# A third output buffer for the Mamba scan, room for it from constants moved into a dead tile, and the first scan unit one place sooner in the issue table

## The chip, the cores and the metric

One core of a Trainium2 chip runs the whole kernel. The metric is device microseconds for one execution; the kernel before takes 7903.27 us (median of 3 runs, 7898.69 to 7904.27).

## The reference, cut to what matters

Four layers follow each other on an image of 2 x 64 x 96 x 96 in fp32. Layer 0 is a non-local attention block over all 9216 positions. Layer 1 is a depthwise and pointwise convolution followed by one Mamba over the 9216 positions of each image. Layer 2 runs two bidirectional Mambas, first along the columns, then along the rows, each with a linear map and a residual. Layer 3 is a dynamic 3 x 3 filter. The Mamba of layers 1 and 2 is this, per sequence:

```python
xz = jnp.einsum('nld,ed->nle', u, p['in_proj_w'])
x, z = jnp.split(xz, 2, axis=-1)
x = silu(conv1d(x) + conv_b)                      # 4 taps, depthwise
dt, Bm, Cm = jnp.split(x @ x_proj_w.T, [4, 20], axis=-1)
dt = softplus(dt @ dt_proj_w.T + dt_proj_b)
def step(h, inp):                                 # 16 states for each of 128 channels
    dA = jnp.exp(dt_t[:, :, None] * A)
    h = dA * h + dt_t[:, :, None] * B_t[:, None, :] * x_t[:, :, None]
    return (h, jnp.einsum('nds,ns->nd', h, C_t))
y = (ys + x * p['Dp']) * silu(z)
out = y @ out_proj_w.T                            # plus the residual
```

## The kernel before, in words

Layer 0 (`layer0_direct`) runs alone, to about 2660 us. At its beginning, on idle engines, `prepare` builds the tables and the weights of the first Mamba with the tile `scratch_tile` as scratch. Layers 1 and 2 then run as one stream of 120 units (`layers1_2`, `Mamba.run`). A unit is 768 positions of one image and one direction: 24 units for layer 1 (two images of 12, with a carried state), 96 for layer 2, in pairs of a forward and a backward unit which share their norm and end in one common tail. In the list of units, numbered from 0, layer 2 begins at 24, and the even unit of a pair is the forward one.

**A unit's work.** Its preparation is: norm (`norm_centre` in layer 1 only, `norm_square`, `norm_mean`, `norm_root`, `norm_scale`, `norm_affine`), `conv`, `conv_read`, `gate_mm`, `gate_read`, `silu` (which switches ACT's function table and back), `step_mm`, `step_read`, `step_exp`, then on POOL `step_kept`, `step_sum`, `step_dt`, `step_u`, and `step_write`, which writes the rows of `dt` and `dt*x` to DRAM. `c_mm` and `c_read` make `C`. The scan has 16 steps. A step takes two of the 16 turns of one half of the positions: SP reads its rows back (`read`, L846, five steps ahead, six buffers `spread`), ACT makes the decay (`decay`, L853, three steps ahead, nine buffers `h`), DVE makes the inputs for two steps at once from `spread` and `B` (`inputs`, L863, into `place`), DVE scans (L878, or L874 with a carried state), POOL multiplies by `C` (L879), and PE gathers into the PSUM bank `y` (L885 for the direct term, L888 for the steps) two or three steps later. `B` is one PSUM bank, made anew by `shared` (L857) for each half of a unit: before step 0 and at step 6 for step 8.

**The end of a unit.** `y_half` (L892) copies the first half of `y` from PSUM into the tile `yg`, `y_read` (L895) the second, POOL gates it (`y_gate`, L898). `tail_0` and `tail_1` (L671, one for each half) multiply the `yg` of all units of a group by the output weights on PE, and `tail_read` (L921 or L924) reads the sum. In layer 2 the tail of a pair reads the `yg` of both units, and comes 25 and 26 steps after the start of the second. All PSUM products but `B`, `y` and `place` go through one buffer, tag `m` of the pool `ssm_m`, named `mm` or `conv` in the profile.

**What sets the order.** The order is written out by hand (`manual_schedule`): in `run`, `n` counts steps, 16 to a unit, and for each `n` the pieces of all units whose offset in `PIECES` falls there are issued. So unit `i` has its `conv` at step 16i - 27, its `step_write` at 16i - 6, its scan at 16i to 16i + 15, its `y_half` at 16i + 10. The pieces of unit 0 before its scan are issued ahead of the loop. Within a step the row read, the decay, the inputs, the scan and the gathers are issued first, then the pieces in `reads`, then the others. `other` issues, twice a unit, the leftover pointwise chunks of layer 1 and the weights of later Mambas. Each engine works its own queue in this order.

**Memory.** The pool `ssm` has two buffers per tag unless `bufs` is given. `k.xa`, the big image tile, is dead during layers 1 and 2, and a `Carver` cuts scratch and weights from it. `turned` (1 KB per partition) and `dtw` (2.5 KB) lie in the constant pool.

Of the kernel before, what the change touches and what calls it, by code (L numbers as in the profile page):

```python
# [19 lines left out]
FP = mybir.dt.float32  # L20
# [5 lines left out]
P = 128  # L26
# [45 lines left out]
def setup(ctx, tc, x, cols, mats, dtw):  # L72

    nc = tc.nc
    const = ctx.enter_context(tc.tile_pool(name="const", bufs=1))
    big = ctx.enter_context(tc.tile_pool(name="big", bufs=1))
    k = SimpleNamespace(tc=tc, nc=nc, const=const)

    k.mats = const.tile([P, NMAT], FP, name="mats")
    k.cols = const.tile([P, NCOL], FP, name="cols")  # L80
    k.dtw = const.tile([DT_RANK, NMAMBA * P], FP, name="dtw")
    first = MAT_AT["g_b"][1]
    nc.scalar.dma_start(out=k.mats[:, :first], in_=mats[:, :first])
    nc.scalar.dma_start(out=k.cols, in_=cols)
    nc.scalar.dma_start(out=k.mats[:, first:], in_=mats[:, first:])
    nc.scalar.dma_start(out=k.dtw, in_=dtw)
    k.xa = big.tile([P, L], FP, name="xa")
    k.xb = big.tile([P, L], FP, name="xb")


    half, step = L // 2, L // 6
    own, other = rows_of(0), rows_of(1)
    for i in range(0, half, step):
        nc.sync.dma_start(out=k.xa[own, i : i + step], in_=x[own, i : i + step])
        nc.sync.dma_start(out=k.xb[other, half + i : half + i + step], in_=x[own, half + i : half + i + step])
    nc.sync.dma_start(out=k.xa[other, :half], in_=x[other, :half])
    nc.sync.dma_start(out=k.xb[own, half:], in_=x[other, half:])
    nc.sync.dma_start(out=k.xa[:, half:], in_=x[:, half:])

    k.ident = const.tile([P, P], FP, name="ident")  # L100
    make_identity(nc, k.ident)

    k.mean_c = const.tile([P, P], FP, name="mean_c")
    nc.vector.memset(k.mean_c, 0.0)
    for b in range(B):
        nc.vector.memset(k.mean_c[rows_of(b), rows_of(b)], 1.0 / C)

    k.mean = const.tile([P, 1], FP, name="mean")
    nc.vector.memset(k.mean, 1.0 / C)
    k.mean = k.mean.to_broadcast([P, P])  # L110
    k.eps = const.tile([P, 1], FP, name="eps")
    nc.vector.memset(k.eps, EPS)
    k.minus = const.tile([P, 1], FP, name="minus")
    nc.vector.memset(k.minus, -1.0)

    k.col = lambda name, rows=slice(0, P): k.cols[rows, COL_AT[name][0] : COL_AT[name][1]]
    k.mat = lambda name, rows=slice(0, P): k.mats[rows, MAT_AT[name][0] : MAT_AT[name][1]]
    return k
# [409 lines left out]
def mamba_tables(k, pool):  # L528

    nc = k.nc
    G = P // 8
    t = SimpleNamespace()

    t.member = pool.tile([P, 8], FP, name="member")
    nc.vector.reduce_sum(t.member, k.ident.rearrange("p (g i) -> p i g", i=8), axis=AX.X)
    t.group = pool.tile([P, 2, G], FP, name="group")
    for j in range(2):
        nc.vector.reduce_sum(t.group[:, j], k.ident.rearrange("p (g i) -> p g i", i=8), axis=AX.X)  # L540

    t.turned = pool.tile([P, G, G], FP, name="turned")
    two = t.group.rearrange("p j g -> p (j g)")
    for n in range(G):
        nc.vector.tensor_copy(t.turned[:, n], two[:, G - n : 2 * G - n])

    pair = pool.tile([P, 2, P], FP, name="pair")
    nc.vector.tensor_copy(pair, k.ident.unsqueeze(1).to_broadcast([P, 2, P]))
    pair = pair.rearrange("p j c -> p (j c)")
    t.gather = [pair[:, P - 8 * n : 2 * P - 8 * n] for n in range(G)]  # L550

    t.centre = pool.tile([P, 2, C], FP, name="centre")
    for j in range(2):
        nc.vector.tensor_add(t.centre[:, j], k.ident[:, :C], k.ident[:, C:])
        nc.vector.tensor_scalar_add(t.centre[:, j], t.centre[:, j], -1.0 / C)
    t.centre = t.centre.rearrange("p j c -> p (j c)")
    return t


def scratch(t, pool):  # L560

    t.placed = pool.tile([P, D_STATE, 8], FP, name="placed")
    t.rates = pool.tile([P, P // 8, P // 8], FP, name="turned_rates")


def mamba_weights(k, w, pool, product, tables, i):

    nc = k.nc  # L570
    G = P // 8


    a = pool.tile([P, D_STATE], FP, name=f"A{i}")
    nc.scalar.activation(a, k.col(f"A_log{i}"), AF.Exp)
    nc.vector.tensor_scalar_mul(a, a, -1.0)
    nc.vector.tensor_mul(
        tables.placed,
        tables.member.unsqueeze(1).to_broadcast([P, D_STATE, 8]),
        a.unsqueeze(2).to_broadcast([P, D_STATE, 8]),  # L580
    )
    p = product(tables.placed.rearrange("p s i -> p (s i)"), tables.group[:, 0], P, G)
    yield
    nc.vector.tensor_mul(tables.rates, tables.turned, p.unsqueeze(1).to_broadcast([P, G, G]))  # L584
    w.rates = pool.tile([P, G], FP, name=f"rates{i}")
    nc.vector.reduce_sum(w.rates, tables.rates, axis=AX.X)
    in_w = k.mat(f"in_w{i}")
    if i:
        nc.vector.tensor_scalar_mul(in_w, in_w, k.col(f"norm_w{i}"))
    yield  # L590
    conv_w = k.col(f"convd_w{i}")
    w.taps = pool.tile([P, D_CONV, P], FP, name=f"taps{i}")
    for j in range(D_CONV):
        p = product(conv_w[:, j : j + 1].to_broadcast([P, P]), k.ident, P, P)
        yield
        nc.vector.tensor_mul(w.taps[:, j], in_w[:, :P], p)
        yield
    x_w = k.mat(f"x_w{i}")
    low = pool.tile([DT_RANK, P], FP, name=f"low{i}")
    p = product(x_w[:, :DT_RANK], k.ident, DT_RANK, P)  # L600
    yield
    nc.vector.tensor_copy(low, p)
    yield
    p = product(low, k.dtw[:, bass.ts(i, P)], P, P)
    yield
    w.step = pool.tile([P, P], FP, name=f"step{i}")
    nc.vector.tensor_copy(w.step, p)
    w.direct = pool.tile([P, P], FP, name=f"direct{i}")
    nc.vector.tensor_scalar_mul(w.direct, k.ident, k.col(f"Dp{i}"))
    bc = pool.tile([P, 2, D_STATE, 8], FP, name=f"bc{i}")  # L610
    for j in range(2):
        at = DT_RANK + j * D_STATE
        nc.vector.tensor_copy(bc[:, j], x_w[:, at : at + D_STATE].unsqueeze(2).to_broadcast([P, D_STATE, 8]))
    w.gate_w = in_w[:, P:]
    w.bc = [bc[:, j].rearrange("p s i -> p (s i)") for j in range(2)]
    w.conv_b, w.dt_b = k.col(f"convd_b{i}"), k.col(f"dt_b{i}")
    w.out_w = k.mat(f"out_w{i}")
    yield


class Mamba:
# [33 lines left out]
    def product(self, lhsT, rhs, m, n):  # L655
        p = self.ps_m.tile([P, 2 * NB], FP, tag="m", name="mm")[:m, :n]
        self.nc.tensor.matmul(p, lhsT=lhsT, rhs=rhs, start=True, stop=True)
        return p
# [229 lines left out]
            self.nc.tensor.matmul(self.y, lhsT=self.t.gather[n], rhs=rhs, start=False, stop=stop)  # L888

    def y_half(self, u):  # L890
        u.y = self.work("yg")
        self.nc.scalar.copy(u.y[:, :HALF], self.y)  # L892

    def y_read(self, u):
# [72 lines left out]
    def run(self, units, first, n_first, other):  # L967


        for u in units:  # L970
            u.dtu, u.h = {}, {}
        steps = [(u, s) for u in units for s in range(self.STEPS)]
        at = lambda n: steps[n] if 0 <= n < len(steps) else None
        reads = ("y_half", "norm_square", "norm_root", "conv_read", "gate_read", "step_read", "c_read", "tail_read")

        table = [[] for _ in range(self.STEPS)]
# [16 lines left out]
        for n in range(begin, len(steps) + end + 1):  # L993
# [5 lines left out]
            if at(n):  # L999
                u = at(n)[0]  # L1000


                if s % 2 == 0:
                    self.inputs(u, s)
                    self.inputs(u, s + 1)
                self.scan(u, s)
                if s == 6:
                    self.shared(u, 1)
                if s == 14 and at(n + 2):
                    self.shared(at(n + 2)[0], 0)  # L1010
            if n == -1:
                self.shared(units[0], 0)
            for late in self.lates(s):
                if at(n - late):
                    self.gather(*at(n - late))
            for late in (False, True):
                for is_late, offset, name in table[s]:
                    i = (n - offset) // self.STEPS
                    if is_late == late and (0 if n >= 0 else 1) <= i < len(units):
                        getattr(self, name)(units[i])  # L1020
                if s in self.OTHER and n >= 0 and not late:
                    next(other, None)


def prepare(k, scratch_tile, ps, tag):
# [5 lines left out]
        return p  # L1031

    k.tables = mamba_tables(k, k.const)
    scratch(k.tables, Carver(scratch_tile))
    k.weights = [SimpleNamespace() for _ in range(NMAMBA)]
    for _ in mamba_weights(k, k.weights[0], k.const, product, k.tables, 0):
        pass
# [2 lines left out]
def layers1_2(k, pre):  # L1040
# [12 lines left out]
    with ExitStack() as stack:  # L1053
# [12 lines left out]


        carver = Carver(k.xa)
        scratch(k.tables, carver)

        def joined(which, lin_w, to):

# [239 lines left out]
```

## Time and profile before

The page gives the span of the profiled execution as 7904.9 us. Busy times over that span, and the costliest rows of layers 1 and 2:

| engine or row | count | busy us (share) or mean ns |
|---|---|---|
| PE | 24578 | 7033.6 (89%) |
| DVE | 5524 | 6744.4 (85%) |
| ACT | 6953 | 5205.2 (66%) |
| POOL | 3146 | 4723.5 (60%) |
| scan L878, DVE | 1536 | 1738 ns |
| scan with carry L874, DVE | 768 | 1003 ns |
| inputs L863, DVE | 1920 | 951 ns |
| product with C L879, POOL | 1920 | 1818 ns |
| decay L853, ACT | 3840 | 607 ns |
| gather L888, PE | 7680 | 508 ns |
| read of rows L846, DMA | 3840 | 384 KB each |

The shares over the whole span mix two regimes. Until 2660 us, in the attention, DVE is busy in 6 tenths and POOL hardly at all; in layers 1 and 2 DVE, POOL and the DMA engines show 8 to 9 tenths, and the DMA engines move 315 to 351 GB/s. So a stage has to be looked at by itself. The page's row for a group gives its busy time, the mean of one, and then the idle time of its engine just before such instructions and who ended most of it. An engine's idle time counts for the end only if it is the engine that the others wait for.

### The profile page before, as it was taken

Reading aid. Unit: us, or ns where it says so; the run is one execution under the profiler, and the core shown is the slowest. Engines: PE = TensorE matmul, PEld = TensorE weight load, DVE = VectorE, ACT = ScalarE, POOL = GpSimd, SP = SyncE. Lnnn points to the kernel's source line nnn. Section 1 sums busy time; section 2 is a strip of 40 time slices with the busy share of each in tenths; the row PEclk is TensorE's granted clock in tenths of the full one; section 3 lists DMA queues with packets and bytes.
Section 4 is the critical chain, followed back from the end, with each engine's and each line's share of the span. In section 5 each row is a group of like instructions: output and inputs, shape, how many; then the busy total and the mean of one; then the engine's idle time right before and its main releaser. Section 6 shows DMA issues by size and latency. Waiting matters only on the chain. (4 is left out here: it accounts for less than half of the span.)

```text
span 7904.9 us, 82275 instructions
## 1 busy us (share of the span) xinstructions
PE 7033.6 (89%) x24578; PEld 3098.9 (39%) x24578; DVE 6744.4 (85%) x5524; ACT 5205.2 (66%) x6953; POOL 4723.5 (60%) x3146
## 2 busy tenths in 40 slices
PE   9999999999999798888888888888888888888887
PEld 3333333333333244444444444444444444444443
DVE  6666666666666499999999999999999999999999
ACT  4444444444444587777777777777777777777774
POOL 0000000000000299999888889889889999999995
PEclk9999999999999899999999999999999999999999
DMA  1000000000000299999889899999999999999995
GB/s 43 1 1 1 1 1 1 3 5 5 5 3 5 105 330 322 328 325 329 321 325 333 315 331 334 332 329 337 330 325 351 345 348 347 336 350 342 344 342 209
DMA packets 593806, 1726.06 MB, mean 218 GB/s; under 512 B 65988, under 2 KB 67140, under 8 KB 592840
## 3 DMA queue, kind: packets, MB, share of 16 engines
q1 hardware_dynamic: 591904, 1717.68, 60.4%
q8 instruction: 196, 3.21, 0.2%
q10 hardware_dynamic: 1448, 3.05, 0.1%
q14 instruction: 258, 2.11, 0.1%
HBM read 1522.68 MB, written 197.79 MB: 218 GB/s over the span
## 5 line engine op out<-in xcount | busy, mean ns | idle before, releaser
L879 POOL TENSOR_TENSOR h<-h,C 128x768 f32<-128x768 f32 x1920 | 3454.0, 1818 | 339.2 <-DVE h L878 304.6
L888 PE MATMUL y<-h,pair 128*128 128x384 f32 x7680 | 2803.3, 508 | 135.1 <-POOL h L879 134.5
L878 DVE TENSOR_TENSOR_SCAN h<-h,place 128x768 f32<-128x768 f32 x1536 | 2606.9, 1738 | 10.8 <-ACT h L853 10.7
L888 PEld LDWEIGHTS y<-h,pair 128*128 128x128 f32 x7680 | 1499.1, 199 | 1335.4 <-POOL h L879 297.7
L311 ACT ACTIVATE e<-f_exp 128x1536 f32<-128x1536 f32 x864 | 1206.4, 1448 | 1224.4 <-PE f_exp L301 1224.4
L853 ACT ACTIVATE h<-spread,xa 128x384 f32<-128x384 f32 x3072 | 1722.5, 607 | 395.0 <-DMA spread<-rows 363.4
L367 DVE TENSOR_TENSOR acc_e<-acc_e,e 128x1536 f32<-128x1536 f32 x792 | 1390.2, 1755 | 683.5 <-ACT e L311 644.6
L863 DVE TENSOR_TENSOR place<-spread,B 128x768 f32<-128x768 f32 x1920 | 1735.0, 951 | 199.6 <-PE B L857 126.7
L340 POOL TENSOR_TENSOR xa<-xa,t_att 64x512 f32<-64x512 f32 x36 | 45.3, 1259 | 2612.0 <-ACT t_att L338 2612.0
L318 PE MATMUL y_att<-e,xb 128*64 128x512 f32 x5184 | 1243.6, 601 | 0.0
L301 PE MATMUL f_exp<-theta,phi 64*128 64x512 f32 x5184 | 1234.5, 607 | 1.0 <-DVE xb L284 0.5
L301 PEld LDWEIGHTS f_exp<-theta,phi 64*128 64x128 f32 x5184 | 466.9, 186 | 754.1 <-issue 460.2
L874 DVE TENSOR_TENSOR_SCAN h<-h,state,place 128x384 f32<-128x384 f32 x768 | 716.4, 1003 | 0.0
L318 PEld LDWEIGHTS y_att<-e,xb 128*64 128x64 f32 x5184 | 341.5, 136 | 830.5 <-issue 829.2
L853 ACT ACTIVATE h<-spread,rates 128x384 f32<-128x384 f32 x768 | 433.8, 608 | 90.6 <-DMA spread<-rows 72.8
L885 PE MATMUL y<-raw,xa 128*128 128x384 f32 x384 | 219.0, 659 | 217.2 <-ACT yg L895 189.8
L671 PE MATMUL mm<-raw,xa 128*128 128x384 f32 x768 | 290.6, 502 | 86.0 <-ACT xb L924 85.9
L766 ACT ACTIVATE raw<-conv,cols 128x768 f32<-128x768 f32 x120 | 108.2, 901 | 280.3 <-PE conv L761 218.9
L806 POOL TENSOR_TENSOR kept<-dtu,kept 128x768 f32<-128x768 f32 x120 | 218.2, 1818 | 100.1 <-ACT kept L799 99.8
L761 PE MATMUL conv<-xn,xa 64*128 64x384 f32 (+3 forms) x1536 | 270.2, 490 | 6.9 <-DVE xa L584 3.0
L892 ACT COPY yg<-y 128x384 f32<-128x384 f32 x120 | 57.4, 478 | 290.9 <-PE mm L671 199.4
L857 PE MATMUL B<-raw,xa 128*128 128x384 f32 x384 | 170.7, 526 | 83.9 <-DVE place L863 83.9
(206 smaller groups left out, 5412.2 us busy)
## 6 DMA issues: line engine op xcount, KB each, us to landing
spread<-rows SPq DMA_DIRECT2D x3840, 384.0 KB, 5.6
rows<-dtu SPq DMA_DIRECT2D x240, 768.0 KB, 6.4
image<-pre SPq DMA_DIRECT2D x11, 384.0 KB, 2.3
xb<-image SPq DMA_DIRECT2D x11, 384.0 KB, 6.7
xa<-in_x SPq DMA_DIRECT2D x1, 2304.0 KB, 22.3
out<-xa ACTq DMA_DIRECT2D x7, 240.0 KB, 2.0
out<-xa SPq DMA_DIRECT2D x1, 1200.0 KB
xa<-in_x SPq DMA_DIRECT2D x3, 384.0 KB, 10.9
```

The costliest lines, as they stand in the source:

```text
L301: nc.tensor.matmul(fs[j // 3][:, bass.ts(j % 3, NB)], lhsT=phi[at, bass.ts(m // 2, P)], rhs=theta[at, bass.ts(i, NB)], start=True, stop=True,)
L311: nc.scalar.activation(e, f, AF.Exp)
L318: nc.tensor.matmul(y[rows_of(m % 2)], lhsT=g[:, m, :], rhs=es[j // 3][:, bass.ts(j % 3, NB)], start=m < 2, stop=m >= KEYS - 2,)
L367: nc.vector.tensor_add(acc, acc, e)
L671: self.nc.tensor.matmul(o, lhsT=lhsT, rhs=x, start=n == 0, stop=n == len(terms) - 1)
L761: self.nc.tensor.matmul(p3[:, :, o], lhsT=lhsT, rhs=x3[:, :, i], **flags)
L853: self.nc.scalar.activation(h[:, bass.ts(q, HALF)], dt, AF.Exp, scale=u.w.rates[:, n : n + 1])
L863: self.nc.vector.tensor_mul(bx, x, self.B.unsqueeze(1).to_broadcast([P, 2, HALF]))
L874: nc.vector.tensor_tensor_scan(h[:, at], h[:, at], bx[:, at], state[:, q : q + 1], ALU.mult, ALU.add)
L878: nc.vector.tensor_tensor_scan(h[:, way], h[:, way], bx[:, way], 0.0, ALU.mult, ALU.add)
L879: nc.gpsimd.tensor_mul(h2, h2, u.C[:, bass.ts(half, HALF)].unsqueeze(1).to_broadcast([P, 2, HALF]))
L888: self.nc.tensor.matmul(self.y, lhsT=self.t.gather[n], rhs=rhs, start=False, stop=stop)
```

## The change

Three things change together.

1. `yg`, the output of a unit, gets three buffers instead of two, so that `y_half` of a unit takes the buffer of the third unit back.
2. Room for it, 3 KB per partition, comes from the constants. `turned` is no longer kept: `scratch` builds it, once in `prepare` and once more, in the dead `k.xa`, when layers 1 and 2 begin. `dtw` is kept only for the first Mamba; the rest is loaded into `k.xa` by a DMA of its own when layers 1 and 2 begin.
3. The list of units in `run` gets an empty unit after the first. Unit 0 keeps its place, and all others stand 16 steps later, so that less of their preparation is issued ahead of unit 0's scan. `shared` for the first half is issued two steps ahead of a unit also where no unit runs.

```diff
-    k.dtw = const.tile([DT_RANK, NMAMBA * P], FP, name="dtw")
+
+    first_dtw = const.tile([DT_RANK, P], FP, name="dtw")
+    k.dtw, k.dtw_in = lambda i: first_dtw, dtw
...
-    nc.scalar.dma_start(out=k.dtw, in_=dtw)
+    nc.scalar.dma_start(out=first_dtw, in_=dtw[:, :P])
...
-    t.turned = pool.tile([P, G, G], FP, name="turned")
-    two = t.group.rearrange("p j g -> p (j g)")
-    for n in range(G):
-        nc.vector.tensor_copy(t.turned[:, n], two[:, G - n : 2 * G - n])
...
-def scratch(t, pool):
-
+def scratch(k, t, pool):
+
+
+    G = P // 8
+    t.turned = pool.tile([P, G, G], FP, name="turned")
+    two = t.group.rearrange("p j g -> p (j g)")
+    for n in range(G):
+        k.nc.vector.tensor_copy(t.turned[:, n], two[:, G - n : 2 * G - n])
...
-    p = product(low, k.dtw[:, bass.ts(i, P)], P, P)
+    p = product(low, k.dtw(i), P, P)
...
-        u.y = self.work("yg")
+        u.y = self.work("yg", bufs=3)
...
+        units = [units[0], None, *units[1:]]
         steps = [(u, s) for u in units for s in range(self.STEPS)]
-        at = lambda n: steps[n] if 0 <= n < len(steps) else None
+        at = lambda n: steps[n] if 0 <= n < len(steps) and steps[n][0] else None
...
-                if s == 14 and at(n + 2):
-                    self.shared(at(n + 2)[0], 0)
-            if n == -1:
-                self.shared(units[0], 0)
+            if s == 14 and at(n + 2):
+                self.shared(at(n + 2)[0], 0)
...
-                    if is_late == late and (0 if n >= 0 else 1) <= i < len(units):
+                    if is_late == late and (0 if n >= 0 else 1) <= i < len(units) and units[i]:
...
-        scratch(k.tables, carver)
+        scratch(k, k.tables, carver)
+        dtw = carver.tile([DT_RANK, (NMAMBA - 1) * P], FP)
+        nc.sync.dma_start(out=dtw, in_=k.dtw_in[:, P:])
+        k.dtw = lambda i: dtw[:, bass.ts(i - 1, P)]
```

More of the change, by code (lines that the diff above doesn't have):

```diff
@@ L1033, in prepare @@
     k.tables = mamba_tables(k, k.const)
-    scratch(k.tables, Carver(scratch_tile))
+    scratch(k, k.tables, Carver(scratch_tile))
     k.weights = [SimpleNamespace() for _ in range(NMAMBA)]
```

## The prediction

> **What bounds the kernel now.** I first cut the span into stages. The attention of layer 0 ends at about 2660 us, the 24 units of layer 1 scan from 2734.5 to about 3774, the 96 units of layer 2 to about 7780, then comes the last convolution. The diff touches nothing that runs before 2660 except where two constants lie, so only the stages after it count. The view of busy time by stage, for the first and second half of layer 2 (columns: length, then PE, weight loads, DVE, ACT, POOL busy with counts, clock, DMA share, GB/s):
>
> ```profile
> 3774.00:5847.00 2073.00, 1736.68 (x5222) 876.65 (x5221) 1960.93 (x1574) 1565.39 (x2353) 1838.81 (x1082) 0.94 0.92 328
> 5847.00:7780.00 1933.00, 1647.21 (x5044) 839.52 (x5042) 1887.18 (x1504) 1484.03 (x2311) 1793.02 (x1056) 0.96 0.95 344
> ```
>
> DVE is the fullest engine. Without waits a layer-2 unit takes 8 x 5.017 = 40.1 us on it (two products and two scans per 5.017 us in its timeline), and many late units take just that. So what can be won here is DVE's idle time, and the waits of DVE alone in 3774 to 7780 say what it is:
>
> ```profile
> DVE place L863 <- PE B L857: 126.1, 81, 3.6
> DVE h L878 <- ACT h L853: 10.7, 18, 0.9
> DVE xa L596 <- PE mm L657: 7.5, 4, 2.4
> ```
>
> With the small rows the sum is 157 us. In 2950 to 3900, layer 1, DVE is busy 945.45 of 950: nothing to win. Going through DVE's timeline unit by unit, 151 of the 157 us fall in the odd units (the second direction of a pair), nearly all before step 0 or step 8, where `B` is new: 116.3 us in the first 25 pairs (4.65 each), 41.0 in the last 23 (1.8 each).
>
> Why is `B` late? PE works in order, so I asked what it and ACT wait for in the same stretch:
>
> ```profile
> ACT yg L892 <- PE mm L671: 199.4, 47, 4.8
> PE mm L671 <- ACT xb L924: 85.9, 46, 2.0
> PE mm L693 <- ACT C L832: 160.6, 46, 6.0
> PE y L885 <- ACT yg L895: 186.6, 74, 5.4
> ```
>
> 47 times, once per pair, ACT's `y_half` stands still because the third `yg` takes the buffer that `tail_0` still reads. Pair 50/51 by timeline, ACT, then PE, then DVE:
>
> ```profile
> 4935.37 0.48 ACT L892 COPY yg<-y 128x384 f32<-128x384 f32 x1 [4.58 <-PE mm L671]
> 4941.10 1.58 ACT L924 ACTIVATE xb<-mm,cols 64x768 f32<-64x768 f32 x1
> ```
>
> ```profile
> 4942.74 1.56 PE L671 MATMUL mm<-raw,xa 128*128 128x384 f32 x4 [1.93 <-ACT xb L924]
> 4946.71 0.81 PE L857 MATMUL B<-raw,xa 128*128 128x384 f32 x2
> 4958.66 1.09 PE L693 MATMUL mm<-sq,mean 64*128 64x384 f32 x4 [4.69 <-ACT C L832]
> 4970.08 0.91 PE L857 MATMUL B<-raw,xa 128*128 128x384 f32 x2
> ```
>
> ```profile
> 4947.56 1.83 DVE L863 TENSOR_TENSOR place<-spread,B 128x768 f32<-128x768 f32 x2 [1.82 <-PE B L857]
> 4957.00 1.75 DVE L878 TENSOR_TENSOR_SCAN h<-h,place 128x768 f32<-128x768 f32 x1 [0.94 <-ACT h L853]
> 4971.03 1.83 DVE L863 TENSOR_TENSOR place<-spread,B 128x768 f32<-128x768 f32 x2 [2.24 <-PE B L857]
> ```
>
> Read down, it is one chain: late `yg`, late tail read, late step product, late `B`, waiting DVE.
>
> **The skill.** "PSUM — Partial Sum Buffer", section "Engine vs sequencer instructions", says that ACT, DVE and POOL queues are strict FIFO and that matmuls start and complete in program order; the chain above agrees. "Perfetto Trace Analysis", "Optimization Strategy", says a gap repeating on the engine that should be saturated can mean too few buffers; 47 equal waits agree. "ScalarE activation tables: per-element evaluation and per-set limits", "What a function is on this engine", gives 1283 ns for a table load; the trace has 1.28 us. "TensorE: Matmul & The Clock Gate", "What's actually happening", says that an idle array falls to half clock; the trace shows 0.50 in 2708 to 2720 as layer 1 starts.
>
> **Part 1, three yg buffers.** In an even unit `y_half` would take the buffer of a unit whose tail ended a unit earlier, so it waits only for the gather before it. That ends at 4931.71 and the copy can start then, 3.7 us sooner than 4935.37. Behind it on ACT stand the table load, silu and second load (1.28 + 1.48 + 1.28), two decays (1.12), then the tail read. New times: copy to 4932.2, silu and loads to 4936.3, decays to 4937.4; the tail's last matmul ends at 4937.39 as before, so the tail read runs 4937.5 to 4939.1 instead of to 4942.68. It frees the one PSUM buffer of the step product. PE has finished its gathers at 4940.82 and starts the product then, not at 4942.74: 1.9 us, the idle time in the PE row (85.9/46 = 1.87 on average). `B` moves from 4946.71 to 4944.8, ready at 4945.7, just when DVE wants it (4940.64 + 5.02 = 4945.66). The wait of 1.82 goes.
>
> In the odd unit ACT reads the step product from 4942.4 instead of 4944.87, 2.5 us sooner. From there to the read of `C` (4957.83) ACT has no idle time, and its decays start 3.7 us or more after their rows landed, by the ends of the DMA packets, so all of it can move up by 2.5. `C` frees the PSUM buffer for the norm's mean; then come `y_read`, four gathers, the conv and `B`, all back to back on PE: second `B` ready at 4968.5 instead of 4971.0. DVE, early by 1.8 + 0.9, would want it at 4965.9. So DVE still waits there, but resumes 2.5 us sooner than before. Per pair DVE gains what `B` gains, 1.9 to 2.5 us (I take 2.3), but no more than its waits. Summed pair by pair with that cap: 57.5 us in the first 25 pairs and 36 in the last 23, 94 together (81 with 1.9, 99 with 2.5). The upper end, were the odd unit's waits to go wholly, is 157. Layer 1 has no such wait: every unit ends with its own tail, so two buffers suffice.
>
> **Part 2, the constants.** `turned` is built twice: 16 more copies of 0.167 us, 2.7 at most, on DVE after 2663.83, where it idles 70.7 us. `dtw` comes by a second small DMA on SP, between the last image load (2666) and the first row write (2703.16); it is read first in unit 7 or later. Both cost nothing.
>
> **Part 3, unit 0 sooner.** DVE's start now:
>
> ```profile
> 2734.53 1.83 DVE L863 TENSOR_TENSOR place<-spread,B 128x768 f32<-128x768 f32 x2 [70.70 <-ACT h L853]
> 2736.27 3.73 DVE L874 TENSOR_TENSOR_SCAN h<-h,state,place 128x384 f32<-128x384 f32 x4
> ```
>
> The first read of unit 0's rows is issued at 2707.99 and lands about 4.8 us later (median of these DMAs), but ACT reaches the first decay at 2727.20 only, behind the norm of unit 2 and conv, silu and step of unit 1. With the new table those come later: step 0 lands near 2712.8, step 1 some 2.0 us on (786 KB at 390 GB/s), the first scan goes at 2715.8, 20.5 us sooner. The unit lasts as before, its last product on POOL ending at 2779.79 - 20.5 = 2759.3.
>
> Now unit 1. Its preparation used to run ahead; now POOL reaches it only behind unit 0's last product: kept, sum, gate, dt, u, 5 x 1.81 = 9.05, to 2768.4. Row write to first read was 4.83 (2703.16 to 2707.99), to 2773.2; landing 4.8, to 2778.0. In ACT's order two decays (1.2) come next, then unit 2's step read (1.7, to 2780.9), which frees the PSUM buffer for the centring of unit 4, and behind that on PE stands unit 1's `B`: 2.4 us at full clock, 4.6 at half, to 2783.3 or 2785.5. Two products (1.8) and the scan starts at 2785 to 2787.3, against 2779.59 now (DVE's timeline). So the empty unit reopens a gap of about 27 us where 20.5 were won: a loss of 6, between 0 (nothing stands behind the step read) and 9. Layer 1 has no idle DVE time to give it back.
>
> **Sum.** 7903.3 - 94 + 6 = 7815.
>
> **Rivals.** (a) All of layer 2's waits go: because PE gaps shrink it also keeps its full clock, and `B` catches up. 7903 - 150 + 6, about 7760 to 7785. For it: late pairs already run at 40.1 with DMA share 0.95. Against: 4.65 us a pair is twice the shift I find. (b) Half the gain: the second `B` is really held by gathers that wait for POOL (row "PEld y L888 <- POOL h L879: 165.4"; POOL is 93% busy in the second half), so only the step 0 waits (50 us) go. 7903 - 50 + 8, about 7860. (c) Slower: ACT, freed, only waits for rows instead ("ACT h L853 <- DMA spread<-rows: 349.2", DMA at 0.92 to 0.95), the waits for `B` stay, and the front gap costs 20 or more, as PE at half clock makes conv and step of units 1 and 2 late as well: 7920 to 7930. Against it: the decays in the odd units start well after their rows.
>
> **Numbers.** Main case 0.62 (7795 to 7840), (a) 0.2, (b) 0.12, no change within 0.2% 0.02, (c) 0.04. Faster 0.94, same 0.02, slower 0.04. The range takes in the main case with both ends of x and of the front, and most of (a) and (b): 7770 to 7862.
>
> **What would show it.** Right: "ACT yg L892 <- PE mm L671" is gone; "PE mm L671 <- ACT xb L924" nearly gone; DVE's waits for `B` fall to 40 to 70 us and stand before step 8 of odd units only; DVE starts near 2715 and has a second gap of about 27 us near 2758 to 2785. Wrong: waits for `B` unchanged though the `yg` wait is gone (another cause), or below 20 us (the shift feeds on itself), or no second gap.

## The result, and the profile after

The changed kernel takes 7868.49 us (median of 4 runs, 7858.85 to 7873.33), the kernel before on the same footing 7903.77: ratio 0.9952, 95% interval 0.9934 to 0.9969. It is faster by 35 us, where 88 were forecast, and 6 us beyond the range of 7770 to 7862.

The three-buffer change did to the first wait what was said. The waits of DVE alone in layer 2 of the changed kernel (3778 to 7745 us; the source lines of the `Mamba` class are three higher than before, so L853, L857, L863 are now L856, L860, L866; columns: total us, times, longest):

```profile
DVE place L866 <- PE B L860: 91.0, 52, 3.6
DVE h L881 <- ACT h L856: 12.4, 19, 1.5
DVE xa L599 <- PE mm L660: 6.5, 4, 2.2
```

All waits together are 117.5 us, down from 157. Before step 0 of odd units nothing is left of 50.3 us. But before step 8 of odd units there are now 84.5 us, up from 71.7. By halves: in the first 25 pairs the waits fell from 116.3 to 76.2 us, in the last 23 they did not fall at all, 41.0 to 41.3. (These sums are of all units; the odd ones alone had 112.8 and 38.6 before. Layer 2's last scan ended at 7823 us, not near 7780, which changes none of them.)

ACT's and PE's waits in the same stretch:

```profile
ACT h L856 <- DMA spread<-rows: 420.0, 623, 4.1
ACT yg L895 <- PE y L891: 86.4, 93, 1.8
```

```profile
PE mm L696 <- ACT C L835: 214.3, 46, 6.4
PE y L888 <- ACT yg L898: 173.2, 51, 5.3
PE mm L674 <- ACT dtu L796: 1.0, 2, 0.8
```

The wait of `yg` for the tail (199.4 us) is gone and so is PE's for the tail read (85.9): before the products of L674 PE now waits 1.0 us. In their place ACT waits 71 us longer for rows, and PE 54 us longer for the read of `C`. The busy time by stage, halves of layer 2:

```profile
3783.00:5814.00 2031.00, 1732.29 (x5217) 878.61 (x5216) 1955.79 (x1571) 1567.76 (x2351) 1838.54 (x1082) 0.94 0.92 335
5814.00:7745.00 1931.00, 1652.34 (x5048) 844.33 (x5047) 1887.90 (x1504) 1486.65 (x2312) 1794.61 (x1056) 0.95 0.95 345
```

The first stretch is 42 us shorter, the second is as long as it was (the cut between them is the start of unit 72).

Pair 50/51 in the changed kernel, ACT then PE then DVE (it starts at 4893.11, before at 4905.52):

```profile
4918.78 0.48 ACT L895 COPY yg<-y 128x384 f32<-128x384 f32 x1 [0.95 <-PE y L891]
4928.90 0.62 ACT L856 ACTIVATE h<-spread,xa 128x384 f32<-128x384 f32 x1 [1.13 <-DMA spread<-rows]
4929.55 0.90 ACT L795 ACTIVATE dtu<-mm,cols 128x768 f32<-128x768 f32 x1
...
4935.86 3.09 ACT L717 COPY xn<-xb 64x768 f32<-64x768 f32 x2
4938.98 0.84 ACT L718 ACTIVATE sq<-xn 128x768 f32<-128x768 f32 x1
...
4942.48 0.78 ACT L835 COPY C<-mm 128x768 f32<-128x768 f32 x1
```

```profile
4927.68 1.45 PE L674 MATMUL mm<-raw,xa 128*128 128x384 f32 x4
4943.31 1.65 PE L696 MATMUL mm<-sq,mean 64*128 64x384 f32 x4 [4.51 <-ACT C L835]
4944.90 1.65 PE L888 MATMUL y<-raw,xa 128*128 128x384 f32 x2
4946.34 7.05 PE L891 MATMUL y<-h,pair 128*128 128x384 f32 x16
4956.05 0.91 PE L860 MATMUL B<-raw,xa 128*128 128x384 f32 x2
```

```profile
4957.00 1.83 DVE L866 TENSOR_TENSOR place<-spread,B 128x768 f32<-128x768 f32 x2 [3.56 <-PE B L860]
```

PE's step product no longer waits and the first `B` is there in time. But ACT stops at 4928.90 for rows, just ahead of the read of the step product. Between that read and the read of `C` (L835) stand the copies and the square of a later norm (L717, L718). PE stands 4.51 us for `C`, about as long as before, then runs slowly (1.65 us for a mean and a direct term that take 0.91 at full clock). DVE waits once, for longer.

The front (the start of layer 1) is much as forecast. DVE at the start of layer 1 and at the empty unit:

```profile
2711.37 0.96 DVE L866 TENSOR_TENSOR place<-spread,B 128x768 f32<-128x768 f32 x1 [46.33 <-DMA spread<-rows]
...
2782.58 1.83 DVE L866 TENSOR_TENSOR place<-spread,B 128x768 f32<-128x768 f32 x2 [27.26 <-DMA spread<-rows]
```

Unit 0 starts 23 us sooner, a gap of 27.3 us opens behind it, and unit 1 starts at 2782.6 instead of 2777.9.

### The profile page after: what moved, and what is told of

Read it like the earlier page. It is cut to its first block, busy times and chain, and to the rows that moved or that the text cites. A ratio compares the mean times of both kernels' runs of the same rounds, so it can differ in the third digit from the quotient of the medians.

```text
span 7868.9 us, 82287 instructions
## 1 busy us (share of the span) xinstructions
PE 7028.5 (89%) x24578; PEld 3101.9 (39%) x24578; DVE 6742.2 (86%) x5540; ACT 5212.2 (66%) x6953; POOL 4726.6 (60%) x3146
## 4 chain that ended last, share of the span: by engine, by line
DMA 11%; issue 11%; PE 9%; POOL 7%; ACT 7%; DVE 6%; SPq 1%; DVEq 0%; ACTq 0%; POOLq 0%
DMA spread<-rows 8%; PE y L891 5%; POOL h L882 5%; DMA rows<-dtu 3%; ACT h L856 3%; DVE place L866 3%; DVE h L881 2%; PE conv L764 1%; PE y L888 1%; POOL dtu L815 1%; PE mm L674 1%; DVE xa L1217 1%; PE mm L696 1%; POOL dtu L819 1%; ACT xn L717 0%
## 5 line engine op out<-in xcount | busy, mean ns | idle before, releaser
L856 ACT ACTIVATE h<-spread,xa 128x384 f32<-128x384 f32 x3072 | 1726.0, 607 | 474.6 <-DMA spread<-rows 429.8
L866 DVE TENSOR_TENSOR place<-spread,B 128x768 f32<-128x768 f32 x1920 | 1728.5, 945 | 167.7 <-PE B L860 92.8
L856 ACT ACTIVATE h<-spread,rates 128x384 f32<-128x384 f32 x768 | 433.5, 608 | 92.4 <-DMA spread<-rows 82.0
L696 PE MATMUL mm<-sq,mean 64*128 64x384 f32 x288 | 100.9, 792 | 233.9 <-ACT C L835 222.9
L674 PE MATMUL mm<-raw,xa 128*128 128x384 f32 x768 | 279.7, 487 | 1.2 <-ACT dtu L796 1.0
L809 POOL TENSOR_TENSOR kept<-dtu,kept 128x768 f32<-128x768 f32 x120 | 218.6, 1822 | 59.2 <-ACT kept L802 57.5
L860 PE MATMUL B<-raw,xa 128*128 128x384 f32 x384 | 172.2, 530 | 90.9 <-DVE place L866 90.9
```

Of the source, the lines that this page charges most:

```text
L674: self.nc.tensor.matmul(o, lhsT=lhsT, rhs=x, start=n == 0, stop=n == len(terms) - 1)
L856: self.nc.scalar.activation(h[:, bass.ts(q, HALF)], dt, AF.Exp, scale=u.w.rates[:, n : n + 1])
L866: self.nc.vector.tensor_mul(bx, x, self.B.unsqueeze(1).to_broadcast([P, 2, HALF]))
```

## The experiments

Three theories for the missing gain were put against each other. **A**: on ACT the read of the step product stands behind the decay of the next unit's first step, and that decay can't start before rows that have to be written to DRAM and read back. **B**: on ACT the copies and the square of a later pair's norm (the pair after the next) stand ahead of the reads of `C` and `y`, and PE, idle till then, has direct term, gathers, conv and `B` left to do. **C**: POOL's products hold the gathers, so that nothing on ACT matters.

Times "into the pair" are counted from DVE's first inputs of the even unit. "The first pairs" are those that begin with units 44 to 72, "the last pairs" those with 76 to 116; their figures are medians.

### Buffers alone, front alone

```diff
# buffers alone: the changed kernel, less
-        units = [units[0], None, *units[1:]]
# front alone: the changed kernel, with
-        u.y = self.work("yg", bufs=3)
+        u.y = self.work("yg")
```

With the buffers alone, `shared` for step 0 is issued as in the kernel before. Expected of the buffers alone:

> The changed kernel without the empty unit in the list; three yg buffers and the moved constants stay. Theory (front and buffers are separate; in the trace of after the front loses 4.7 us and layer 2 wins 40): 7868.5 - 4.7 = 7864, 7860 to 7867, DVE's waits in layer 2 at 117 as in after, the second gap of DVE near 2758 gone, one gap of 70 us at the start. Rival (the empty unit also shifts the leftover work `other` by a unit, and this makes part of layer 2's gain): waits in layer 2 at 130 or more, 7875 or slower.

and of the front alone:

> The changed kernel with two yg buffers; the empty unit and the moved constants stay. Theory: layer 2 as before (157 us of DVE waits, the wait of y_half for the tail back, 4.2 us 47 times), front loses 4.7: 7903.8 + 4.7 = 7908, 7904 to 7912. Rival (the front is a gain on its own and was hidden): below 7895.

Measured on one chip, against 7905.35 before: buffers alone 7857.41, ratio 0.9939 (0.9926 to 0.9953); front alone 7913.48, ratio 1.0008 (1.0002 to 1.0015). So the buffers win 48 us, the front loses 8 (2 to 12 by its interval), and the two add up to the 35 of the result within their intervals. Both times lie just outside what was expected, as the front costs rather more than the 4.7 us of one trace. Counted from the end of layer 0's work on DVE, unit 1 starts after 114.1 us in the kernel before, 118.2 in the changed one and 121.8 with the front alone; the gap is 26 to 29 us in every trace with the empty unit. The rival for the front, a hidden gain, is out, and so is the one that has the empty unit help layer 2: without it the waits there are 105 us, not more than 117. One trace is a rough measure of these waits: front alone has 141 us where 157 were expected, and in the trace of the buffers alone the last 23 pairs have 29.4, not 41.3.

### The step read ahead of the decay

```diff
-        (-19, "step_read"),
+        (-20, "step_read"),
```

> The changed kernel with step_read one step sooner in the table (-20 instead of -19), so that on ACT it stands ahead of the decay of the next unit's first step, whose rows land at about 35.3 us after the start of the even unit. Theory A (the gain was stopped by this decay: the read of the step product waits behind it in ACT's queue, which is why it moved up by 1.9 us in the first half of layer 2 and 0.3 in the second where y_half moved by 3.5 and 2.7): step read at 36.1 instead of 37.1, second B 1 to 2 us sooner, waits before step 8 from 84 to 45 to 60: 7830 to 7850. Theory B (ACT's norm square ahead of the read of C and y holds the second B, and PE's packed work after it): second B no more than 1 us sooner, 7855 to 7868. Theory C (POOL's products hold the gathers before the second B): unchanged, 7866 to 7872.

7871.65 us, ratio 0.9955 (0.9942 to 0.9969): nothing gained. Theory A as I had written it missed by 20 us or more, and only the range of C takes the number in; C is decided by the two runs that follow. The step read did move, by 1.8 us in the last pairs (35.0 us into the pair instead of 36.8). But it then stands 1.6 us for its product from PE, the decay comes behind it, at 36.6 instead of 34.2, and the read of `C` moves by 0.7 only (47.9 from 48.6). Two items of one queue have changed places, and ACT waits for PE where it waited for rows.

### Rows written two steps sooner

```diff
-        (-11, "step_dt"),
-        (-9, "step_u"),
-        (-6, "step_write"),
+        (-13, "step_dt"),
+        (-11, "step_u"),
+        (-8, "step_write"),
```

> The changed kernel with step_dt, step_u and step_write two steps sooner in the table (-13, -11, -8). Theory A (row write and read back, 5.7 + 4.2 us after step_u, set when the decay of the odd unit's first step can start, and this holds ACT): rows of the odd unit land 4 to 5 us sooner, near 30 to 31, the read of the step product is held by PE only (36.1), the second B 1 to 2 us sooner; the front also wins 1.8 because y_gate comes behind step_dt: 7825 to 7850. Theory C (POOL is the holder): POOL does dt and u ahead of products, gathers come later, 7870 to 7895. Theory B: 7855 to 7868.

7843.91 us, ratio 0.9919 (0.9906 to 0.9933): 25 faster than the changed kernel (7868.49, ratio 0.9952). POOL ends `step_u` 3.5 us sooner (21.8 instead of 25.3), the odd unit's first rows land 2 us sooner (33.3 instead of 35.3), less than the 4 to 5 I had expected. In the last 23 pairs DVE's waits fall from 41 to 12 us; in the first 25 they stay, 73.9. So the rows' landing is what stopped the gain in the second half of layer 2. For the first half this run does not tell: POOL does `dt` and `u` ahead of products there, PE's waits for products grow from 66.8 to 229.3 us, `y_half` comes 0.5 us later in the first pairs, and the step read, no longer held by rows, waits 0.9 us for PE. C as written there, a loss, is out. The front did not win its 1.8 us: its gap is 28.8.

Where the landing holds ACT is plain in pair 88/89, which starts at 6506.49 before and at 6469.45 after. ACT before:

```profile
6540.13 0.88 ACT L924 ACTIVATE xb<-mm,cols 64x768 f32<-64x768 f32 x1
...
6541.01 2.12 ACT L853 ACTIVATE h<-spread,xa 128x384 f32<-128x384 f32 x4
6543.03 0.89 ACT L792 ACTIVATE dtu<-mm,cols 128x768 f32<-128x768 f32 x1
```

and after:

```profile
6500.11 0.88 ACT L927 ACTIVATE xb<-mm,cols 64x768 f32<-64x768 f32 x1
...
6504.16 0.61 ACT L856 ACTIVATE h<-spread,xa 128x384 f32<-128x384 f32 x1 [2.07 <-DMA spread<-rows]
6507.24 0.62 ACT L856 ACTIVATE h<-spread,xa 128x384 f32<-128x384 f32 x1 [2.46 <-DMA spread<-rows]
6507.76 0.88 ACT L795 ACTIVATE dtu<-mm,cols 128x768 f32<-128x768 f32 x1
```

From the start of the pair the tail read moves from 33.6 to 30.7, 3 us sooner, and the step read from 36.5 to 38.3: later. SP shows why. It issues the odd unit's rows to DRAM at 6494.81 and can issue the first read of them only at 6500.57, 0.1 us after the semaphore of the write's landing (6500.47):

```profile
6494.81 0.80 SPq L828 DMA_DIRECT2D rows<-dtu  x2
6500.57 8.88 SPq L849 DMA_DIRECT2D spread<-rows  x12
```

PE, done sooner with what comes before, waits for `C` the longer, 2.91 us before (the row of L693 at 6555.30) and this after:

```profile
6519.96 1.65 PE L696 MATMUL mm<-sq,mean 64*128 64x384 f32 x4 [6.17 <-ACT C L835]
6521.54 1.65 PE L888 MATMUL y<-raw,xa 128*128 128x384 f32 x2
```

### The norm behind the reads of C and y

```diff
-        (-51, "norm_centre"),
-        (-49, "norm_square"),
-        (-47, "norm_mean"),
-        (-45, "norm_root"),
+        (-47, "norm_centre"),
+        (-45, "norm_square"),
+        (-45, "norm_mean"),
+        (-44, "norm_root"),
...
-    OTHER = (3, 5)
+    OTHER = (4, 5)
```

> The changed kernel with the norm of the next pair later in the table: norm_centre at -47, norm_square and norm_mean at -45, norm_root at -44 (from -51, -49, -47, -45), and OTHER at steps 4 and 5 instead of 3 and 5. On ACT the square then stands behind the reads of C and y, not ahead of them, and on PE the mean behind the first gathers. Theory B (three copies and squares of 3.2 to 4.0 us in ACT's queue hold C and y_read, PE idles 4.5 us for them and then has direct term, gathers, conv and B to do without a break; this set the second B): y_read and the direct term 2.5 to 4 us sooner, waits before step 8 from 84 to 20 or less: 7790 to 7815. Theory A alone (only the rows' landing holds ACT): no more than 20 us, 7850 to 7868. Theory C (POOL's products hold the gathers): 7860 or more.

7797.49 us, ratio 0.9869 (0.9854 to 0.9884), as theory B said. The read of `C` comes 4.1 us sooner in the first pairs (46.0 from 50.1 us into the pair), 2.9 in the last (45.7 from 48.6), and the waits before step 8 of odd units fall from 84.5 to 23.9 us, a little short of the 20 expected. DVE's waits for `B` in all of layer 2 (91.0 us in the changed kernel):

```profile
DVE place L866 <- PE B L860: 29.8, 22, 3.2
```

Pair 88/89 of this kernel starts at 6410.68. ACT, with the norm's copies and square now behind the two reads, and PE there:

```profile
6455.95 0.78 ACT L835 COPY C<-mm 128x768 f32<-128x768 f32 x1
...
6457.79 0.46 ACT L898 COPY yg<-y 128x384 f32<-128x384 f32 x1
...
6459.78 1.66 ACT L717 COPY xn<-xb 64x768 f32<-64x768 f32 x2
6461.47 0.84 ACT L718 ACTIVATE sq<-xn 128x768 f32<-128x768 f32 x1
```

```profile
6458.30 0.91 PE L888 MATMUL y<-raw,xa 128*128 128x384 f32 x2 [3.29 <-ACT yg L898]
6459.05 4.44 PE L891 MATMUL y<-h,pair 128*128 128x384 f32 x8
6463.42 0.91 PE L696 MATMUL mm<-sq,mean 64*128 64x384 f32 x4
...
6469.78 0.91 PE L860 MATMUL B<-raw,xa 128*128 128x384 f32 x2
```

The direct term starts 47.6 us into the pair instead of 52.1, and `B` ends at 60.0, where DVE needs it at 60.2. The next pair starts 80.3 us after this one, twice 40.1: no wait is left in this pair. The first gathers take 4.44 us for two steps, and that is the clock: the trace shows it granted at half from 6459.47 to 6462.88, and POOL had ended the products that they read 2.1 us or more before (median of the last pairs). So PE still falls to half clock here, in 14 of the 21 last pairs as soon as the direct term.

The edit moves two things, ACT's copies and square behind the reads and PE's mean behind the gathers. They were not tried apart, but the times tell which counts: in the changed kernel the direct term starts 0.25 us after the end of the copy of `y` that it waits for, so the mean ahead of it can have cost no more than that, and the copy comes 4.1 us sooner in the first pairs (47.7 from 51.8).

### The norm later, with two buffers

> norm_later with two yg buffers. Theory B (two causes add: the yg wait makes the first B late, the norm the second): the waits before step 0 of odd units stay near 47, those before step 8 fall below 25; 7840 to 7860, that is 40 to 55 slower than norm_later. Rival (with the norm out of the way ACT has the slack to take the yg wait, so the third buffer is worth nothing): within 10 of norm_later.

7823.89 us, ratio 0.9901 (0.9887 to 0.9914): 26 slower than with three, which is neither forecast, but nearer to the first. The waits before step 0 are back at 33.1 us, those before step 8 are at 13.8. ACT's wait for the tail is back in full:

```profile
ACT yg L895 <- PE mm L674: 200.5, 47, 4.8
```

So the third buffer is still worth something, about half of its 48 us, though it takes away the same 200 us of ACT's waiting. Why it is about half was not tried.

### Everything but the empty unit

The last two leave out the empty unit: the norm later, and the norm and the rows sooner together.

> norm_later without the empty unit in the list. If the front's cost is its own (8 to 11 us in the runs so far): 9 faster than norm_later, 7780 to 7805. If the front cost depends on the norm (which now comes later for unit 1 as well): the same as norm_later.

> b3_norm_nogap with step_dt, step_u and step_write two steps sooner too. Theory A and B (rows and norm are two separate holds): another 10 to 20 sooner, waits of DVE in layer 2 below 25, 7765 to 7785. If the norm alone was left: no change from b3_norm_nogap.

7785.45 us, ratio 0.9854 (0.9839 to 0.9869), 12 faster than with the empty unit; and 7763.12, ratio 0.9825 (0.9812 to 0.9839), the fastest of all and just below its range. So the rows, worth 25 us on the changed kernel, are worth 22 behind the norm as well, in both halves (waits 27.4 to 10.7 and 12.5 to 0 us). Layer 2 of the fastest kernel, in one stage (its last scan ends at 7677):

```profile
3780.00:7710.00 3930.00, 3365.51 (x10393) 1654.81 (x10392) 3904.94 (x3123) 3081.59 (x4710) 3664.70 (x2163) 0.99 0.95 345
```

DVE is busy 3904.94 of 3930 us. The waits before step 8 of odd units are gone, 10.7 us of waits are left in the layer, and PE's clock is 0.99 where the changed kernel had 0.94 and 0.95. Here POOL begins to set PE's pace, which theory C had looked for in the changed kernel: in the last pairs the gather of step 3 starts 0.17 us after its product ends, in the changed kernel 3.7 us after. PE's waits for products in this kernel, 66.8 us in the changed one:

```profile
PE y L891 <- POOL h L882: 234.8, 394, 2.0
```

What is left to win there has to come from DVE's work itself.

## Why the prediction was wrong, point by point

**What bounds the kernel: right.** DVE's waits were what could be won, and the fastest kernel got nearly all 157 us of them. What the prediction takes from the Trainium skill ("Perfetto Trace Analysis", "Optimization Strategy") speaks of a gap on the engine that should be saturated, which is DVE; the 47 waits were on ACT, and their 199 us were worth 48.

**The first chain: right, and of the size given.** `y_half` moved up by 3.5 us in the first pairs (4.2 in pair 50, 3.7 worked out), PE's wait for the tail read went from 85.9 us to nothing, the first `B` came 2.4 us sooner (1.9 worked out), and the waits before step 0 fell from 50.3 to 0.

**The step that failed: "all of it can move up by 2.5".** I had looked at the decays of pair 50 and found them 3.7 us or more behind their rows. The ones that matter are the two of the odd unit's first step, just ahead of the step read. In every trace whose row write stands where it did, the last packet of their rows lands 34.7 to 35.5 us into the pair. Before, the second of them started at 38.6 in the first pairs and at 36.8 in the last. After, it starts at 36.5 and 36.2, and waits for rows in 12 of 15 first pairs and in all 21 last ones. So there were 2.1 us to move in the first pairs and 0.6 in the last. The step read moved by 1.9 and 0.6, and `C` by 1.8 and 0.4. In pair 50 the step read moved by 2.9, as much as the argument needed: I had one pair of the first half stand for both halves.

**The term that was mis-sized: 2.3 us a pair.** The second `B` came 1.4 us sooner in the first pairs and 0.4 later in the last. From step read to direct term most of the shift was kept in the first pairs (1.9, 1.8 for `C`, 1.6); 0.2 us was lost on PE between direct term and `B`, and 0.7 in the last pairs. So the sum of 57.5 + 36 became 40.1 + (-0.3), in the waits of the two traces; with the buffers alone it was 40.2 + 11.6. Of the signs named, the `yg` wait, the step 0 waits and the second gap came true; the waits for `B` stayed at 91.0 us, above the 40 to 70 given.

**What was lost on PE.** PE ended its work ahead of the mean sooner, but `C` did not come sooner by as much, so PE's gap grew: in the last pairs from 2.84 to 4.39 us. The odd units whose direct term took 1.65 us, not 0.91, rose there from 15 to 20 of 21, and the time from direct term to conv by 0.4 us. The gathers' input was not what made it: POOL had ended the products of the first four steps 3.7 us or more before the gathers that read them (medians of the last pairs). It was the clock. In the last 23 pairs the trace has it at half for 157 us before and 205 after; front alone, with two buffers, has 147, buffers alone 198. In the first 25 pairs the two sides differ less clearly (242 and 198 against 249 and 256). In the kernel with norm and rows moved the gap is 1.5 us and no direct term is slow. The Trainium skill ("TensorE: Matmul & The Clock Gate", "What's actually happening") says that an idle array falls to half clock after an idle window of about 3.4 us; here shorter gaps did it too: in the kernel before, 12 of the 15 slow direct terms have 2.0 to 3.2 us as the longest gap ahead of them.

**The front: right in sign and nearly in size, with some luck.** 6 us of loss were worked out, 0 to 9 given as bounds; 8 were measured with the front alone, and 10 to 12 between pairs of kernels with and without it, a little over the upper bound. In the traces compared above, unit 1 starts only 4 to 8 us later, so part of the 10 to 12 is not accounted for. Of the chain, POOL's end and `B` came nearly as written: the row write of unit 1 at 2766.8 (2768.4 worked out), centring 2.92 us at half clock, `B` ready at 2782.5 (2783.3 to 2785.5). In between, the rows of step 0 landed at 2775.3, not 2778.0, and its decays did not wait for them: ACT's own queue, busy without a break from 2768.6, and the step product from PE set the step read, which ended at 2778.0 (2780.9). The gap of 27.3 us (27 worked out) agrees because both its ends came some 2.5 us sooner.

**The constants: no cost found.** The second set of copies for `turned` ends at 2665.1 on DVE, 46 us ahead of its first inputs, and the DMA for `dtw` is issued at 2667.4, ahead of the first row write.

**The rivals.** (a), where PE keeps its full clock, did not come with this change (0.94 and 0.95 in layer 2); 7763 and a clock of 0.99 took norm and rows moved as well, and no empty unit. (b) has the right size, 7860, and half of its reason: only the step 0 waits went. But its holder was the wrong engine. Moving ACT's norm freed the second `B`, so POOL's products did not hold it in this kernel. (c) named the row wait, which is what capped the second half (ACT's waits for rows rose from 349 to 420 us), but gave it too much: it stopped the gain and cost nothing more.

## What to carry to other kernels

A wait that is taken away moves what stands behind it in the queue only up to the next item that waits for something else: before counting on a shift, look at every item between the freed one and the one that matters, in each stage, and ask how long its own input has been there. On a queue that is full, the order of the items can then decide more than the buffers: here a table edit that put the norm behind two reads was worth some 65 us on top of the change's 35 (ratio 0.9869 against 0.9952). A piece of work started a place sooner won nothing here, because the next one's preparation is a serial chain behind it.

## What the runs showed of the hardware that I had not expected

The way of 1.5 MB of rows to DRAM and back takes longer in the full stream than I had thought: from the issue of the write to the first issue of the read 5.3 us in the last pairs of the changed kernel (5.8 in pair 88), against 3.3 for units 0 and 1 at its front (4.8 and 4.3 for the same units in the kernel before). Ending the write's producer 3.5 us sooner brought the rows 2 us sooner.

An engine that is not the bound lost speed by being early: with three buffers PE finishes sooner what comes before its gap, and in the last 23 pairs its clock is at half for 198 to 205 us instead of 147 to 157. In all ten traces each stretch of half clock in layer 2 lasts 3.4 us or two or three times that. A stretch that begins near the end of a gap falls on the work behind it, as on the gathers of pair 88 in the kernel with the norm later.
